# Mixed token pieces kept as 16-bit integers for the up stage, up-weight blocks one chunk later, second element's integers one chunk sooner

## The chip, the core and the metric

The kernel runs on one core of a Trainium2 chip. The time of a run is the device time of one execution in microseconds (us). The core has a matrix engine (TensorE, PE in the profile; its weight loads are shown as PEld), three elementwise engines (VectorE = DVE, ScalarE = ACT, GpSimd = POOL), and SyncE (SP), which in this kernel does hardly more than issue DMA transfers. The data sits in SBUF (128 partitions), matmul results in PSUM banks, everything large in DRAM (HBM).

## The reference, cut to what matters

Sixteen sequences ("elements") of 512 tokens, 512 features each. A cross attention comes first and its result is added to x; then a quantized feed-forward network follows, whose hidden size is 1536:

```
x = x + attention(layernorm(x), ctx)
h = act_qdq(layernorm(x))                      # 16-bit integers times one scale for the whole tensor
up   = act_qdq(h @ lpbq_dequant(w_up).T)       # weights: 4-bit integers, one scale per block of 32
gate = act_qdq(h @ lpbq_dequant(w_gate).T)
sig  = fixed_qdq_u16(sigmoid(gate))            # multiples of 1/65536
gate = act_qdq(gate * sig)
o    = act_qdq(gate * up)
x = x + o @ lpbq_dequant(w_down).T

act_qdq(x): scale = max(max|x| / 32767, 1e-12); round(x / scale), clipped to 16 bits, times scale
```

Each `act_qdq` needs the largest magnitude of its whole tensor before the first element can be rounded. This is why the network cannot be run in one pass: gate has to be finished over all elements before its integers exist, and so on.

## The kernel before, in words

There are five stages: attention (to 992 us), gate (to 1559), up (to 2120), a short turn in which the scales of o are found (to 2160), and down (to the end).

**Pieces.** The integers of the tokens have 16 bits, more than a matmul takes in one go at full speed. So `Tokens` cuts a tile of 128 features by 512 tokens (one of four, `d`, of an element) into three `Pieces`: `hi` (the integer rounded to a multiple of 256, `split_high`, L705), `lo` (the rest) and `mix` (`hi` minus a multiple of `lo`; both in `split_low`, L707 to L711). Weights are likewise kept as three pieces, made once and stored in DRAM. The product is made from three passes: the mixed pieces (`begin`, L769), then after one scaling of the sums in PSUM on ACT (`divide`, L775) the low and high pieces (`rest`, L725).

**Chunks and steps.** The gate and the up stage each have 96 chunks: sixteen elements by six chunks `f` of 256 hidden features. A chunk is 24 matmuls, 8 in `begin` and 16 in `rest`. One `step(i)` writes the order by hand for PE, DVE, ACT and POOL:

```python
nxt.begin()              # PE: 8 matmuls of chunk i+1
chunks[i - 1].out(...)   # ACT: copy sums to t, SyncE: store t
before()                 # ACT: gate integers (up stage)
nxt.divide()             # ACT
middle()
chunks[i].rest()         # PE: 16 matmuls of chunk i
after()
```

The sums have three PSUM buffers, the tile `t` three; two further PSUM banks ("tp") are for transposes. SyncE is not in the hand-written order: its order of issues is planned at compile time, from when the planner takes each DMA to be ready, and SyncE then issues in that order, one after the other, each when what it waits for has come.

**Gate stage** (the loop over `b` and `f` after `chunks[0].divide()`). The tokens of element b+1 are got ready while element b is multiplied: `load` brings the rows of x (one element earlier, at its f=2), `normalize` (POOL, at its f=4), then, in element b, `quantize` (L828 to L832: ACT makes the integers `xi`, one DMA transposes them into the integer tile `xq`, another, issued right behind, stores `xq` to DRAM as `xq_d` for the up stage; f=0, for element 1 f=2), the high splits on POOL (f=1, 2), the low splits with the mixes on DVE (f=2, 3, 4). There are two integer tiles `xq`, and two sets of four pieces. Elements 1 to 12 also prepare one block of up weights each (`up_weight`: load at f=0, quantize at f=1, transposes on PE at f=2 and the rest of the split at f=3), and elements 2, 5, 8 and 11 begin one block of down weights (`down_weight`, L844; load at their f=4, quantize at f=5, then three transposing steps in the next element at f=0 to 3). Within one `after`, the down block's step stands ahead of the up block's. Both take one of the two tp banks per step, and a bank is free again when the DVE step L169 of `rest()` of the same turn has read it; `rest()` of one down step is called at the next one.

In this text a gate element is counted from 0. An up block's own four steps start inside element b at the step with f=0; PE runs `after` of a step behind the 16 matmuls of that step, so the transposes of f=2 stand behind the rest of chunk 2 and ahead of the begin of chunk 4.

**Up stage** (the loop over `k`). The elements are taken in the order 15, 14, 0, 1, ... 13: the pieces of 15 and 14 are still in SBUF. For all others the integers come back from `xq_d` (L1041, at f=4 two elements ahead) and are split again during the element before: high on POOL ahead of the step, low and mix on DVE behind it, one `d` in each of f=0 to 3. That makes 56 low splits and 56 mixes. Alongside runs the gate work, per chunk: load gate sums `gt` (L975, seven buffers), integers and sigmoid on ACT (L953, L959), two DVE steps that make the rounded sigmoid and the product p (`times`, L963, L964), its store `p_d` (L982), the product with `t` on POOL (L987), two reductions on DVE (L991 and L792). So SyncE has three transfers of 512 KB in each chunk: `gt` in, `p_d` and `u_d` (the sums of the up product) out. At k=1 the scale of the gate is found, at k=3 (L1062) the scale of p, with a few small steps on ACT and DVE.

Of the kernel before, what the change touches and what calls it, by code (L numbers as in the profile page):

```python
# [9 lines left out]
F32 = mybir.dt.float32  # L10
F32R = mybir.dt.float32r
I32 = mybir.dt.int32
I16 = mybir.dt.int16
# [8 lines left out]
P = 128  # L22
# [31 lines left out]
def tile_xattn_ffn(  # L54
# [16 lines left out]
    nc = tc.nc  # L71
    B, S, D = x.shape
    SK = cx.shape[1]
    FF = w_gate.shape[0]
    ND = D // P
    NF = FF // P
    NQ = S // P
# [7 lines left out]
    dram = ctx.enter_context(tc.tile_pool(name="dram", bufs=1, space=DRAM))  # L85
# [8 lines left out]
    max_x = const.tile([P, B * NQ], F32, name="max_x")  # L94

    xq_d = [dram.tile([P, NQ, ND, P], I16, name=f"xq_{b}") for b in range(B)]

    wg_d, wu_d, wd_d = (dram.tile([P, NF, 3, D], F32, name=f"w{k}_d") for k in "gud")
    x1_d = [dram.tile([NQ, P, D], F32, name=f"x1_{b}") for b in range(B)]
# [22 lines left out]
    class WeightBlock:  # L122
# [13 lines left out]
        def quantize(self):  # L136
            pool, I, tag, nm = self.pool, self.I, self.tag, self.nm
            nb = I // WBLOCK
            wb = self.wt.rearrange("p (n k) -> p n k", k=WBLOCK)
            s = pool.tile([P, nb], F32, tag=f"s_{tag}", name=f"ws_{nm}", bufs=1)  # L140
            nc.vector.tensor_reduce(s, wb, AX.X, ALU.max, apply_absolute_value=True)
            nc.vector.tensor_scalar(s, s, 1.0 / 7.0, SCALE_MIN, ALU.mult, ALU.max)
            r = pool.tile([P, nb], F32, tag=f"r_{tag}", name=f"wr_{nm}", bufs=1)
            nc.vector.reciprocal(r, s)
            q = pool.tile([P, I], I16, tag=f"q_{tag}", name=f"wq_{nm}", bufs=1)
            qb = q.rearrange("p (n k) -> p n k", k=WBLOCK)
            nc.vector.tensor_tensor(
                qb, wb, r.unsqueeze(2).to_broadcast([P, nb, WBLOCK]), ALU.mult
            )
            nc.vector.tensor_scalar(q, q, 7.0, -8.0, ALU.min, ALU.max)  # L150
            nc.vector.tensor_tensor(
                wb, qb, s.unsqueeze(2).to_broadcast([P, nb, WBLOCK]), ALU.mult
            )
# [550 lines left out]

        engine.tensor_scalar(as_runs(p.hi, q), q, TO_256, TO_256, ALU.add, ALU.subtract)  # L705

    def split_low(p, q):  # L707
        nc.vector.tensor_tensor(  # L708
            as_runs(p.lo, q), q, as_runs(p.hi, q).bitcast(F32), ALU.subtract
        )  # L710
        nc.vector.scalar_tensor_tensor(  # L711
            out=p.mix, in0=p.lo.bitcast(F32), scalar=-SPLIT, in1=p.hi.bitcast(F32),
            op0=ALU.mult, op1=ALU.add,
        )

    def as_runs(t, q):
        return t if t.shape == q.shape else t.rearrange("p (q t) -> p q t", t=q.shape[-1])
# [21 lines left out]
    with ExitStack() as gu:  # L739
        ps_mm = gu.enter_context(tc.tile_pool(name="psf_mm", bufs=3, space=PSUM))  # L740
        xpool = gu.enter_context(tc.tile_pool(name="ff_x", bufs=1))
# [3 lines left out]
        class Tokens:  # L745


            def __init__(self, b, nm):
                self.b, self.nm, self.p = b, f"{nm}_{b}", []
                self.q = xpool.tile([P, NQ, ND, P], I16, tag="xq", name=f"xq_{self.nm}", bufs=2)  # L750

            def high(self, d, engine):
                self.p.append(Pieces(xpool, "x", [P, S], 8, f"{self.nm}_{d}"))
                split_high(self.p[d], self.q[:, :, d, :], engine)

            def low(self, d):
                split_low(self.p[d], self.q[:, :, d, :])

        class Chunk:
            def __init__(self, w, x, b, f):  # L760
# [35 lines left out]
        wp = wprep.__enter__()  # L796
# [9 lines left out]
        xs = {0: Tokens(0, "g")}  # L806
# [18 lines left out]
        def quantize(b):  # L825

            xi = wp.tile([P, NQ * D], I16, tag="xi", name=f"xi_{b}")
            nc.scalar.activation(  # L828
                xi, xs[b].x1.rearrange("p q d -> p (q d)"), AF.Copy, scale=r_x
            )  # L830
            nc.sync.dma_start_transpose(xs[b].q.rearrange("p q d t -> p (q d) t"), xi)
            nc.sync.dma_start(xq_d[b], xs[b].q)  # L832


        def up_weight(o):
# [24 lines left out]
        load(1)  # L860
        normalize(1)
        wg.load(range(4, NF))
        nc.sync.dma_start(xq_d[0], xs[0].q)
        nc.vector.tensor_scalar(s_xw, s_x, WHOLE, None, ALU.mult)

        order = [B - 1, B - 2, *range(B - 2)]
        chunks = [Chunk(wg, b, b, f) for b in range(B) for f in range(N2)]
        chunks += [Chunk(wu, b, b, f) for b in order for f in range(N2)]
        xu = {}
# [28 lines left out]
        for b in range(B):  # L898
            for f in range(N2):
                i = b * N2 + f  # L900

                def middle():
                    if f == (0 if b else 2) and b + 1 < B:
                        quantize(b + 1)

                def after():

                    if b == 0:
                        high = {3: ((0, nc.vector), (1, nc.gpsimd), (2, nc.gpsimd)), 4: ((3, nc.vector),)}
                        low = {3: (0,), 4: (1, 2, 3)}  # L910
                    else:
                        high = {k: ((2 * k - 2, nc.gpsimd), (2 * k - 1, nc.gpsimd)) for k in (1, 2)}
                        low = {2: (0, 1), 3: (2,), 4: (3,)}
                    if b + 1 < B:
                        for d, engine in high.get(f, ()):
                            xs[b + 1].high(d, engine)
                        for d in low.get(f, ()):
                            xs[b + 1].low(d)
                    if i > 0:
                        chunks[i - 1].largest(max_g, **size)  # L920
                        chunks[i - 1].largest(top_g)
                    if f == 2 and b + 2 < B:
                        load(b + 2)
                    if f == 4 and b + 2 < B:
                        normalize(b + 2)
                    if f == 0 and 1 <= b <= NF:
                        ups.extend(up_weight(b - 1))
                    if f == 4 and b % 3 == 2 and b < NF:
                        downs.extend(down_weight(b // 3))
                    for jobs in (downs, ups):  # L930
                        if jobs:
                            jobs.pop(0)()
                    if b == B - 1:
                        wu.load((0,) if f == 0 else (2 * f - 1, 2 * f))

                if b == B - 1 and f == 0:
                    wprep.__exit__(None, None, None)
                step(i, None, middle, after)


# [80 lines left out]
        for k in range(NCH):  # L1021
            i, n = NCH + k, k // N2
            f = k % N2

            def before():
                for j in sig[k]:
                    gates[j].sigmoid()

            def middle():
                for j in sig[k]:  # L1030
                    gates[j].sigmoid2()

            def after():
                if k == 0:
                    wu.load((NF - 1,))
                if splits:
                    xu[order[n + 1]].low(f)
                if n + 2 < B and f == ND:
                    b = order[n + 2]
                    xu[b] = Tokens(b, "u")  # L1040
                    nc.sync.dma_start(xu[b].q, xq_d[b])  # L1041
                if n == B - 1:
                    wd.load((0,) if f == 0 else range(max(1, 2 * f - 3), 2 * f - 1), (0,))

            splits = 1 <= n < B - 1 and f < ND
            if splits:
                xu[order[n + 1]].high(f, nc.gpsimd)
            for j in times[k]:
                gate_times(j)
            while multiplied:  # L1050
                gate_rows(multiplied.pop(0))
            step(i, before, middle, None)
            for j in times[k]:
                gate_product(j)
                multiplied.append(j)
            if k == 0:
                chunks[NCH - 1].largest(max_g, **size)
                chunks[NCH - 1].largest(top_g)
            else:
                chunks[i - 1].largest(max_u, **size)  # L1060
            if k == 1:
                m_g = over_all([max_g, top_g], "g")  # L1062
                s_g, r_g = scale_of(m_g[:, 0:1], s_xw, "g")
                nc.vector.tensor_tensor(r_g, r_g, s_xw, ALU.mult)
            if k == 3:


                nc.vector.tensor_copy(m_p, m_g[:, 1:2])
                top = Gate(m_p, 1, "top")
                top.sigmoid()  # L1070
                top.sigmoid2()
                top.times()
                scales_of_p()
                low = small.tile([P, 1], F32, name="low")
                nc.vector.tensor_scalar(low, m_p, P_LEAST * U16_ONE, None, ALU.is_lt)
                nc.gpsimd.iota(first_i, pattern=[[0, 1]], base=0, channel_multiplier=NF)
                nc.vector.tensor_copy(first_row, first_i)
            if k == 0:
                for j in range(3):
                    gate_load(j)  # L1080
            gate_load(k + 3)
            after()

        for j in times[NCH]:
# [45 lines left out]
    with ExitStack() as dn:  # L1130
# [38 lines left out]
        class Unit:  # L1169
# [10 lines left out]
            def fetch(self, g, more=""):  # L1180
                self.q[g] = factors(self.b, self.h, 4 * g, more)
# [139 lines left out]
        with tc.If(nc.values_load(again[0:1, 0:1], min_val=0, max_val=1)):  # L1321
            every = [(b, h, f) for b, h in units for f in range(0, NF, 4)]
            max_p = small.tile([P, len(every)], F32, name="max_p")
            for i, unit_f in enumerate(every):
                p, _ = factors(*unit_f)
# [77 lines left out]
```

## Time and profile before

The median of three runs is 2714.57 us (2711.21 to 2718.05). The profiled execution took 2716.41 us.

| profiled execution | us |
|---|---|
| its time | 2716.41 |
| span, first to last instruction | 2714.6 |
| attention, to 992.0 | 992.0 |
| gate, 992.0 to 1559.4 | 567.4 |
| up, 1559.4 to 2120.2 | 560.8 |
| turn, 2120.2 to 2160.0 | 39.8 |
| down, to the end | 554.6 |

| busy us in the stage | PE | DVE | ACT | POOL | share of the DMA engines |
|---|---|---|---|---|---|
| gate | 546.6 | 416.0 | 234.0 | 285.1 | 0.67 |
| up | 546.9 | 513.6 | 390.9 | 365.5 | 0.85 |
| down | 537.5 | 447.1 | 232.0 | 396.4 | 0.67 |

The first table is read from the begins of the stages in the timeline, the second from the view of windows, which gives the busy time of each engine in a stretch, the clock that was granted to TensorE in it, and what the DMA engines moved. The view of waits lists, for each engine and line, how long it stood idle and whose end released it; the lines of SyncE in it (SPq) are the waits of the queue of DMA issues. A line number is one of the kernel before.

### The profile page before, as it was taken

To read this page: it belongs to the slowest core of one execution; us is meant where nothing else is said; L and a number is where in the kernel's file an instruction comes from. 1 tells how busy PE (TensorE), PEld (TensorE's weight loads), DVE (VectorE), ACT (ScalarE), POOL (GpSimd) and SP (SyncE) were. 2 spreads that over 40 slices of the span, in tenths; PEclk is the share of its full clock that TensorE was granted. 3 is DMA by queue.
4 is the path that set the end of the run, shared out by engine and by line. 5 is a ranking of instruction groups with operands and counts; after the bars stand their busy time and mean duration, and the time that the engine had idled before them with its cause. 6 is when DMAs were issued, how large, how long until landed. Compare 5 with 4: busy or idle time off the path is not lost. (4 is left out here: it accounts for less than half of the span.)

```text
span 2714.6 us, 30451 instructions
## 1 busy us (share of the span) xinstructions
PE 2586.2 (95%) x10934; PEld 1692.6 (62%) x10934; DVE 2067.9 (76%) x2671; ACT 1092.3 (40%) x1182; POOL 1603.8 (59%) x1011
## 2 busy tenths in 40 slices
PE   8899999999999879999999999999999389999999
PEld 4334434333343347787787878777777278788787
DVE  4667766776777557887878579999998678888886
ACT  1221222222222214444444467766766444444443
POOL 4466665655665145556556147777665367777775
PEclk9999999999999989999999999999999799999999
DMA  4011121111111057666666688888888967777773
GB/s 158 15 62 47 66 89 47 47 54 47 47 68 38 16 202 215 213 194 218 213 198 194 221 296 291 277 276 290 283 279 270 362 236 252 249 255 250 250 248 140
DMA packets 264399, 486.85 MB, mean 179 GB/s; under 512 B 47024, under 2 KB 65584, under 8 KB 264240
## 3 DMA queue, kind: packets, MB, share of 16 engines
q1 hardware_dynamic: 264080, 484.31, 52.7%
q8 instruction: 87, 1.43, 0.2%
q14 instruction: 72, 0.59, 0.1%
q0 software_dynamic: 160, 0.52, 0.0%
HBM read 255.66 MB, written 221.25 MB: 176 GB/s over the span
## 5 line engine op out<-in xcount | busy, mean ns | idle before, releaser
L705 POOL TENSOR_SCALAR oh_d<-oq_d 128x512 fp32r<-128x512 int16 x190 | 398.5, 2119 | 156.1 <-DVE oq_d L1193 155.8
L987 POOL TENSOR_TENSOR po<-gt,t_wu 128x1024 f32<-128x1024 f32 x96 | 231.5, 2411 | 242.6 <-DVE gt L964 127.4
L384 ACT COPY ao<-pv 128x512 f32<-128x512 f32 x64 | 37.5, 586 | 505.3 <-PE pv L375 505.3
L308 PE MATMUL qp<-xnT,wq_sb 128*128 128x512 f32 x512 | 236.4, 604 | 0.0
L404 PE MATMUL op<-wo_sb,ao 128*128 128x512 f32 x512 | 232.1, 601 | 0.0
L792 DVE TENSOR_REDUCE max_g<-t_wg 128x1 f32<-128x1024 f32 x96 | 116.8, 1216 | 135.3 <-ACT t_wg L787 135.3
L705 POOL TENSOR_SCALAR xh_g<-xq_g 128x512 fp32r<-128x512 int16 x60 | 121.6, 2046 | 164.4 <-DMA xq_g<-xi 158.5
L769 PE MATMUL mm_wg<-xm_g,wg 128*128 128x512 f32 x768 | 203.8, 408 | 9.3 <-DMA wg<-wg_d 4.6
L1210 PE MATMUL dn_d<-wd,om_d 128*128 128x512 f32 x768 | 194.6, 402 | 18.2 <-DMA wd<-wd_d 6.4
L725 PE MATMUL mm_wg<-xl_g,wg 128*128 128x512 f32 x768 | 208.0, 393 | 0.0
L725 PE MATMUL mm_wg<-xh_g,wg 128*128 128x512 f32 x768 | 205.7, 390 | 0.0
L220 POOL TENSOR_TENSOR rt_q<-rt_q,sin_q 128x512 f32<-128x512 f32 x64 | 81.4, 1272 | 202.5 <-DVE rt_q L217 202.5
L1193 DVE SCALAR_TENSOR_TENSOR oq_d<-pq_d,r_o,uq_d 128x1024 int16<-128x1024 int16 x96 | 128.0, 1333 | 82.0 <-ACT uq_d L1146 82.0
L725 PE MATMUL mm_wu<-xl_u,wu 128*128 128x512 f32 x672 | 185.8, 398 | 2.2 <-ACT mm_wu L775 2.2
L1210 PE MATMUL dn_d<-wd,ol_d 128*128 128x512 f32 x768 | 184.6, 389 | 0.4 <-ACT dn_d L1222 0.4
L1210 PE MATMUL dn_d<-wd,oh_d 128*128 128x512 f32 x768 | 184.5, 389 | 0.0
L1210 PEld LDWEIGHTS dn_d<-wd,om_d 128*128 128x128 f32 x768 | 144.2, 192 | 63.4 <-DVE om_d L711 20.3
L769 PE MATMUL mm_wu<-xm_u,wu 128*128 128x512 f32 x672 | 173.1, 399 | 11.0 <-ACT t_wu L787 6.8
L335 DVE TRANSPOSE_TENSOR_REDUCE mt<-st 128x32 f32<-128x1024 f32 x128 | 151.7, 1224 | 39.1 <-PE st L329 38.9
L725 PE MATMUL mm_wu<-xh_u,wu 128*128 128x512 f32 x672 | 180.1, 390 | 0.0
L308 PEld LDWEIGHTS qp<-xnT,wq_sb 128*128 128x128 f32 x512 | 92.1, 189 | 137.8 <-issue 111.2
L769 PEld LDWEIGHTS mm_wg<-xm_g,wg 128*128 128x128 f32 x768 | 148.4, 196 | 42.9 <-DVE xm_g L711 8.1
(248 smaller groups left out, 5586.1 us busy)
## 6 DMA issues: line engine op xcount, KB each, us to landing
g_d<-t_wg SPq DMA_DIRECT2D x96, 512.0 KB, 3.4
gt<-g_d SPq DMA_DIRECT2D x96, 512.0 KB, 4.5
u_d<-t_wu SPq DMA_DIRECT2D x96, 512.0 KB, 5.8
p_d<-gt SPq DMA_DIRECT2D x96, 512.0 KB, 5.1
p<-p_d SPq DMA_DIRECT2D x96, 512.0 KB, 4.9
u<-u_d SPq DMA_DIRECT2D x96, 512.0 KB, 5.9
xt<-in_x_dram SPq DMA_DIRECT2D x16, 1024.0 KB, 5.3
x<-xt SPq DMA_DIRECT2D x16, 1024.0 KB, 4.3
```

Source lines behind the costliest of these rows:

```text
L220: nc.gpsimd.tensor_tensor(v(t), v(t), sin, ALU.mult)
L308: nc.tensor.matmul(ps, lhsT=wq_sb[:, d, ts(g, P)], rhs=self.xnT[:, d, :], start=(d == 0), stop=(d == ND - 1),)
L335: nc.vector.tensor_reduce(self.mt[:, 2 * i : 2 * i + 2, :NB], self.st[i].rearrange("p h (c j) -> p h c j", j=DK), AX.X, ALU.max, apply_tra ...
L384: nc.scalar.copy(self.ao[:, g, :], pv)
L404: nc.tensor.matmul(ps, lhsT=self.ao[:, g, ts(q, P)], rhs=wo_sb[:, g, :], start=(g == 0), stop=(g == NG - 1),)
L705: engine.tensor_scalar(as_runs(p.hi, q), q, TO_256, TO_256, ALU.add, ALU.subtract)
L725: nc.tensor.matmul(ps[:, j, :], lhsT=lhs(j, i)[k], rhs=rhs(j, i)[k], start=(k == 0 and i == 0), stop=(k != 1 and i == n - 1), skip_group_c ...
L769: nc.tensor.matmul(self.ps[:, j, :], lhsT=lhs(j, d), rhs=self.x.p[d].mix, start=(d == 0), stop=(d == ND - 1), skip_group_check=True,)
L792: nc.vector.tensor_reduce(maxes[:, i : i + 1], self.t, AX.XYZ, ALU.max, **how)
L987: nc.gpsimd.tensor_tensor(flat(g.po), flat(g.tile), flat(c.t), ALU.mult)
L1193: nc.vector.scalar_tensor_tensor(out=oq.rearrange("p f t -> p (f t)"), in0=pq, scalar=r_o, in1=uq, op0=ALU.mult, op1=ALU.mult,)
L1210: nc.tensor.matmul(self.ps[j], lhsT=self.p[f // 2].all()[k][:, f % 2, ts(j, P)], rhs=wd.made[f][k], start=(k == 0 and f == 0), stop=(k != ...
```

## The change

The change has these parts:

- `split_low` gets a flag, and its second instruction becomes `split_mix`. In the up stage the mixes are not computed by DVE any more. In the gate stage `short_mixes` (ACT, f=2 and 3 of each element but the last two) writes the mixed pieces divided by 256 as 16-bit integers into a tile `xn`, which is stored to DRAM (`xn_d`, 512 KB per element). In the up stage `fetch` loads `xn` behind `xq`, and `mix` (ACT, in the middle of the steps f=0 to 3) multiplies it by 256 back into the mixed piece. `xn` has one buffer in each stage.
- The integer tile `xq` has one buffer instead of two.
- The store of `xq` is a method `keep`, called in `after` at f=1 (for element 1 at f=2) instead of right behind the transposing DMA, and not for elements 14 and 15.
- Element 1 is quantized at f=1 of element 0 instead of f=2, and two of its low splits instead of one are made at f=3.
- The up-weight block starts at f=1 instead of f=0, so each of its four steps stands one chunk later.
- The scale of p is found at k=2 instead of k=3.

```diff
-    def split_low(p, q):
+    def split_low(p, q, mix=True):
         nc.vector.tensor_tensor(
             as_runs(p.lo, q), q, as_runs(p.hi, q).bitcast(F32), ALU.subtract
         )
+        if mix:
+            split_mix(p)
+
+    def split_mix(p):
         nc.vector.scalar_tensor_tensor(
             out=p.mix, in0=p.lo.bitcast(F32), scalar=-SPLIT, in1=p.hi.bitcast(F32),
...
-                self.q = xpool.tile([P, NQ, ND, P], I16, tag="xq", name=f"xq_{self.nm}", bufs=2)
+                self.q = xpool.tile([P, NQ, ND, P], I16, tag="xq", name=f"xq_{self.nm}", bufs=1)
...
-            def low(self, d):
-                split_low(self.p[d], self.q[:, :, d, :])
+            def low(self, d, mix=True):
+                split_low(self.p[d], self.q[:, :, d, :], mix)
+            def keep(self):
+                nc.sync.dma_start(xq_d[self.b], self.q)
+            def short_mixes(self, pool, ds):
+                if ds[0] == 0:
+                    self.n = pool.tile([P, ND, S], I16, tag="xn", name=f"xn_{self.nm}", bufs=1)
+                for d in ds:
+                    nc.scalar.mul(self.n[:, d, :], self.p[d].mix.bitcast(F32), 1.0 / 256.0)
+                if ds[-1] == ND - 1:
+                    nc.sync.dma_start(xn_d[self.b], self.n)
+            def fetch(self):
+                nc.sync.dma_start(self.q, xq_d[self.b])
+                self.n = xpool.tile([P, ND, S], I16, tag="xn", name=f"xn_{self.nm}", bufs=1)
+                nc.sync.dma_start(self.n, xn_d[self.b])
+            def mix(self, d):
+                nc.scalar.mul(self.p[d].mix, self.n[:, d, :], 256.0)
...
             nc.sync.dma_start_transpose(xs[b].q.rearrange("p q d t -> p (q d) t"), xi)
-            nc.sync.dma_start(xq_d[b], xs[b].q)
...
-        nc.sync.dma_start(xq_d[0], xs[0].q)
+        xs[0].keep()
...
                 def middle():
-                    if f == (0 if b else 2) and b + 1 < B:
+                    if f == (0 if b else 1) and b + 1 < B:
                         quantize(b + 1)
+                    if f in (2, 3) and b < B - 2:
+                        xs[b].short_mixes(wp, ((0, 1), (2, 3))[f - 2])
...
-                        low = {3: (0,), 4: (1, 2, 3)}
+                        low = {3: (0, 1), 4: (2, 3)}
...
+                    if f == (1 if b else 2) and b + 1 < B - 2:
+                        xs[b + 1].keep()
...
-                    if f == 0 and 1 <= b <= NF:
+                    if f == 1 and 1 <= b <= NF:
                         ups.extend(up_weight(b - 1))
...
             def middle():
                 for j in sig[k]:
                     gates[j].sigmoid2()
+                if splits:
+                    xu[order[n + 1]].mix(f)
...
                 if splits:
-                    xu[order[n + 1]].low(f)
+                    xu[order[n + 1]].low(f, False)
...
-                    nc.sync.dma_start(xu[b].q, xq_d[b])
+                    xu[b].fetch()
...
-            if k == 3:
+            if k == 2:
                 nc.vector.tensor_copy(m_p, m_g[:, 1:2])
                 top = Gate(m_p, 1, "top")
```

More of the change, by code (lines that the diff above doesn't have):

```diff
@@ L96, in tile_xattn_ffn @@
     xq_d = [dram.tile([P, NQ, ND, P], I16, name=f"xq_{b}") for b in range(B)]
+    xn_d = [dram.tile([P, ND, S], I16, name=f"xn_{b}") for b in range(B)]
     wg_d, wu_d, wd_d = (dram.tile([P, NF, 3, D], F32, name=f"w{k}_d") for k in "gud")
```

## The prediction

> **What bounds the kernel now.** I read the page's slices first, of forty 68 us each:
>
> ```profile
> PE   8899999999999879999999999999999389999999
> ...
> DVE  4667766776777557887878579999998678888886
> ...
> DMA  4011121111111057666666688888888967777773
> ```
>
> Gate is slices 15 to 23 (992 to 1559 us), up 24 to 31 (to 2120), down the last nine. In both of the first two PE counts as 90% busy; DVE is at 70% in the gate stage and over 90% in the first half of up, where DMA is above 80%. A busy PE may be a slow one, so I took the begins of the chunks from the timeline. An unhindered chunk (24 matmuls) lasts 5.44 us, an element of six 32.6, and a gate element that also turns one up block 33.1. Up needs 561 us where 96 chunks of 5.44 are 522. The waits of PE, then of SyncE from 1710 to 2100 us (time, times, longest):
>
> ```profile
> PE tp_wu L159 <- issue: 16.1, 4, 4.3
> ...
> PE mm_wu L769 <- ACT t_wu L787: 6.8, 10, 1.3
> ...
> PE mm_wg L769 <- DVE xm_g L711: 4.4, 4, 2.0
> ```
> ```profile
> SPq L975 <- DMA p_d<-gt: 241.3, 65, 5.9
> ```
>
> **Gate.** The wait of 16.1 falls in elements 3, 6, 9 and 12, which turn a down block as well. The timeline of element 3, then two windows (busy of PE, PEld, DVE, ACT, POOL, granted clock, DMA share, GB/s):
>
> ```profile
> 1121.95 0.60 PE L159 MATMUL tp_wd<-ident,wt_wd 128*128 128x128 f32 x4
> ...
> 1125.20 0.69 DVE L169 TENSOR_TENSOR wt_wd<-tp_wd,wt_wd 128x512 f32<-128x512 f32 x1
> ...
> 1125.99 1.09 PE L159 MATMUL tp_wu<-ident,wt_wu 128*128 128x128 f32 x4 [3.44 <-issue]
> ...
> 1126.73 3.76 PE L769 MATMUL mm_wg<-xm_g,wg 128*128 128x512 f32 x8
> ```
> ```profile
> 1126.60:1134.60 8.00, 8.00 (x28) 6.43 (x27) 7.57 (x9) 3.03 (x4) 4.06 (x3) 0.69 0.66 217
> 1140.00:1173.00 33.00, 33.00 (x149) 27.35 (x148) 24.02 (x28) 14.51 (x14) 16.02 (x9) 1.00 0.63 200
> ```
>
> The reader is to see that PE turns a down part at 1121.95, then stands 3.44 us before the up block's turn (both at f=2), whose PSUM bank DVE frees only at 1125.89 (L169: 1125.20 and 0.69), behind the low splits. After it the granted clock is 0.69 and the next chunk takes 7.8 us. The four elements last 40.8, 40.6, 41.8 and 40.3, 163.5 together.
>
> **Up.** SyncE issues the stores and loads of a chunk in one fixed turn:
>
> ```profile
> 1745.70 0.57 SPq L975 DMA_DIRECT2D gt<-g_d  x1
> 1746.36 0.56 SPq L982 DMA_DIRECT2D p_d<-gt  x1
> 1747.02 0.57 SPq L788 DMA_DIRECT2D u_d<-t_wu  x1
> 1751.63 0.57 SPq L975 DMA_DIRECT2D gt<-g_d  x1
> ```
> ```profile
> 1700.00:1800.00 100.00, 98.79 (x428) 79.31 (x427) 98.94 (x97) 71.82 (x71) 73.58 (x31) 1.00 0.82 275
> 2000.00:2100.00 100.00, 96.66 (x407) 73.87 (x405) 86.84 (x86) 68.68 (x68) 60.58 (x26) 1.00 0.81 271
> ```
>
> The gt load waits until the p store issued one turn earlier has landed, since there are seven gt buffers. A turn is (2095.1-1710.5)/65 = 5.92 us, 0.48 over PE's 5.44, 31 us over the 65. DVE made that p some ten us before its store was issued (multiplied at 1865.7, issued 1876.6). And DVE's share falls from 98.94 to 86.84 of 100 while the turn stays as it is: the loop of issues sets the pace, not DVE.
>
> **The change, part by part.** The profiled execution took 2716.4 (span 2714.6), 1.8 above the median 2714.6; the sum starts from 2716.4.
>
> *Up block one chunk later.* Each block moves whole: one load of 256 KB, six DVE instructions of quantizing (3.1 us), four transposes, and after them two on DVE (0.68, 0.69), one on ACT (0.63), one on POOL (1.7) and three stores. At f=2 PE then turns only a down part; the block's turn comes at f=3, where the down block only ends its split, and its bank was freed a chunk before. An element of this kind should take 33.1 plus three down turns of .36 to .5, 34.3: 163.5-4*34.3 = 26 us saved. Bounds: 0 (another wait takes its place) and 26; the 16.1 alone if the slow clock stays. I take 26, since the 33.1 us of a neighbour with a clock of 1.00 is the nearest row. POOL's last step of the block (1.7) now stands behind its normalize (8.3); POOL is busy 16 of 33, so nothing, and 1.7 a block if that cover were gone. SyncE issues the load and the stores 5.4 us later, in a stage where nothing of the chain waits for them.
>
> *Stored integers in the gate stage.* 56 ACT copies f32 to 16-bit: not in the trace; the f32 copies of this size are 0.63, a 16-bit one 0.70, so 39 us in 14 elements on an engine 14.5 of 33 busy, between the division and the next copy of t: nothing; 0.7 each on PE at worst. The 14 stores of 512 KB meet a DMA share of 0.63: nothing. The xq stores move on SyncE from behind the transposing DMA to f=1 or 2, and two fall away: nothing. From element 2 on the single buffer asks that the transposing DMA (f=0) follow the last low split of the element before (f=4, one chunk earlier) and its xq store (f=1): both are done, so nothing.
>
> *Element 1 sooner.* begin(1) is 6.0 us late now, for DVE's mixes. Its ACT quantize at 1013.6 could start at 1009. But with one integer buffer the transposing DMA needs the xq store of element 0 landed (1018.66, behind 24 weight loads), 4 to 5 us later than the ACT step allows: gain eaten. Bounds -6 and +3; I take 0, as the last mix comes out at 1032.3 against 1032.6.
>
> *DVE relief in up.* 56 mixes of 0.90 leave DVE (50.3 us) and 56 go to ACT, of 0.65 each, between the two rows above (4.31 busy per 5.44 chunk, so 4.96 where it falls: hidden, but with 0.5 to spare). The loop of issues is untouched by it: 0. Bounds: 0 and -31 (the whole excess). One chunk of 9.67 in the first split element waits 2.6 for a DVE mix; its 4.2 go, and come back as waiting in the loop.
>
> *Loads of the integers.* Turns with an xq load last 6.00 and the next 6.19, others 5.84: 0.16+0.35 = 0.5 us a load. 14 more of the same 512 KB: +7. Bounds 0.1 and 2.0 each (two turns reached 7.87), +1 to +26. More traffic needs 1.748 MB in 5.44 us, 321 GB/s in such a chunk, under the 362 that slice 34 shows. *One xq buffer:* the fetch waits for the last low split, which the second buffer spares it now. The earliest fetch still lands in time (issued 1730.1, landed 1737.0, POOL's split at 1739.8). Later ones slip: issued at 1872.2 or after, landing 6.4 later, where POOL starts at 1874.2. Taken so for each element, eight loads land 0.4 to 4.6 us after POOL's present start, 26.5 together. p's ten us and 4 to 6 us of lead of gt hide that; without cover, see below. Bunching after it +2.
>
> *Top gate at k=2*: two ACT steps (0.28, 0.29), a table load of 1.28 and small DVE steps stand one chunk sooner, where SyncE's loop has not begun to wait; -2 (0 to -5.4, a chunk).
>
> By the Trainium skill, "DMA: Bandwidth & Descriptors", "Anatomy of one DMA — SWDGE (gpsimd) path", a transfer costs about 2.0 us plus bytes over 436 GB/s; an estimate from it gives 1.2 us of moving for each integer load and +17 instead of +7, though the path named there is not the one used here, and the turns above show 0.5.
>
> Sum: 2716.4-26+0+0+7+2-2 = 2697.4, less the 1.8 to the median: **2696**. Its own range goes two thirds of the way to the bounds of the loads (+1, +26) and of element 1 (-6, +3): 2688 to 2711.
>
> **The rivals.**
>
> *Up is relieved as well.* DVE at 98.9 of 100 in the first half speaks for it; or, with DVE lighter, the planned order puts p's store ahead of the gt load, and the loop loses its waits of up to 5.9. Against: p is ready ten us early, and DVE's share falls with no gain in pace. All 31 gone gives 2716.4-26-31-1.8 = 2658, half of it 2673; about 2666. The Trainium skill, "Perfetto Trace Analysis", "Identifying the Most-Contended Engine", says to optimise the engine of highest occupancy: that is DVE in this stage, and by it this case, 2658, would be the likeliest. The trace does not agree: DVE's share falls by 12 of 100 while the turn stays at 5.92.
>
> *Slower: one buffer of integers.* The late loads pass through POOL and DVE to PE: +26.5, and xn, queued 1.4 us behind xq, holds up the ACT mixes eight times, +11.5; with the 7 of the loads 2716.4-26+26.5+11.5+7-1.8 = 2734 (2722 to 2734). It decides from 2.6 us per element. For it: POOL has 73.6 of 100 busy, ACT 71.8. Against: the leads above.
>
> *New waits in the gate.* The block's quantize ends about 26.0 us into an element, PE wants the turn at 27.1: 1.1 us of room. If DVE's order uses it up, half of the 26 is lost: 2709.
>
> *The early element delays instead*, with its store queued behind the weight loads: +3 at most, inside the first range.
>
> **How the numbers follow.** Forecast .55, up relieved .22, new waits .12, slower .11. 0.3% is 8.1 us (2706.4 and 2722.7), about what a measurement here can tell from no change. Faster holds nearly all of the first two and a little of the third, .78; same .11; slower .11. For the range I leave out about one in ten on each side: up to the start of the slow case, 2722, and down to the middle of the relieved one, 2662.
>
> **What would show it.** Right: no wait of tp_wu in the gate elements 3, 6, 9, 12 and 34 to 35 us for each; begin(1) late as before; SyncE's gt loads still waiting for p's stores, at a turn of 5.9 to 6.0; DVE in up down to 80 of 100. Wrong: a turn near 5.5 (relief), or waits of POOL's high splits or of ACT's mixes for the integers, passed on to PE (slower), or a wait of PE for the block's quantized weights.

## The result and the profile after

The changed kernel takes 2694.59 us (median of four runs, 2691.84 to 2695.72) against 2714.38 for the kernel before; the ratio is 0.9925 with a 95% interval of 0.9908 to 0.9942. The prediction of 2696 lies 1.4 us from it. The gain, however, is in another stage than the one predicted. By the begins of the chunks in the two traces:

| us, profiled executions | before | after |
|---|---|---|
| to the first begin of the gate stage | 992.1 | 993.4 |
| gate stage, to the first begin of the up stage | 567.2 | 568.6 |
| up stage, to the begin of its last chunk | 550.0 | 526.3 |
| from there to the end | 605.3 | 604.0 |
| span | 2714.6 | 2692.3 |

The gate stage, for which 26 us had been promised, is 1.4 us longer. The up stage, for which +7 had been written, is 23.7 us shorter.

**Gate after.** The waits of PE in the changed kernel (engine, tile and line, releaser: us in all, times, longest):

```profile
PE tp_wu L160 <- DVE wt_wu L152: 11.2, 3, 5.1
...
PE tp_wd L160 <- DVE wt_wd L152: 7.1, 4, 2.4
```

The old wait of 16.1 for a PSUM bank is gone, as predicted, and 18.3 us of other waits have come: PE now waits for the quantized weights themselves. The three waits for the up block are in elements 4, 7 and 10, those behind an element with a down block; the four for the down block in elements 3, 6, 9 and 12. Element 3 went from 40.8 to 38.7 us, but element 4 from 33.1 to 37.3, and so on: 6 went from 40.6 to 36.3, 7 from 33.1 to 40.3. The timeline of element 4 shows the order on DVE that does it (start, duration, engine, line, operation; idle time before it and its releaser):

```profile
1157.59 7.62 POOL L706 TENSOR_SCALAR xh_g<-xq_g 128x512 fp32r<-128x512 int16 x4 [9.66 <-PE mm_wg L795]
...
1159.55 1.09 DVE L709 TENSOR_TENSOR xl_g<-xq_g,xh_g 128x512 fp32r<-128x512 int16 x1 [5.83 <-POOL xh_g L706]
...
1165.44 0.68 DVE L142 TENSOR_REDUCE ws_wu<-wt_wu 128x16 f32<-128x512 f32 x1
...
1168.21 0.69 DVE L152 TENSOR_TENSOR wt_wu<-wq_wu,ws_wu 128x512 f32<-128x512 int16 x1
...
1168.96 0.66 PE L160 MATMUL tp_wu<-ident,wt_wu 128*128 128x128 f32 x4 [2.39 <-DVE wt_wu L152]
```

DVE stood idle for 5.83 us ahead of the first low split (L709), which waits for POOL's high split (L706), which started when the transposing DMA landed at 1157.43. The quantizing (L142 to L152) is written behind the two low splits of f=2 and could not start in that gap, though its weights had landed at 1153.69. One chunk earlier, at f=1, there is no low split ahead of it.

The transposing DMA was itself late, and again through the moved block. POOL makes the last piece of the up block of element 3 (L172) behind its normalize (L846); SyncE has the store of that piece ahead of the transposing DMA in its order, and waits 5.6 us for it:

```profile
1138.39 8.27 POOL L846 TENSOR_SCALAR x1t<-x1t,ln_mv,ln_rstd 128x512 f32<-128x512 f32 x4
1146.62 1.30 POOL L172 TENSOR_TENSOR wa_wu<-wt_wu,wt_wu 128x512 f32<-128x512 f32 x1
```
```profile
1147.95 0.32 SPq L861 DMA_DIRECT2D wu_d<-wa_wu  x1
...
1151.85 3.91 SPq L857 DMA_TRANSPOSE xq_g<-xi  x1
```

So the transposing DMA is issued 12.6, 15.5 and 14.2 us into the elements 4, 7 and 10. In 5, 8 and 11 it is issued 10.45 us into the element, the quantizing ends 26.2 us into it, and PE does not wait.

The down block's wait comes from DVE's order as well: its quantizing ends 12.5 to 13.4 us into the element instead of 10.2 to 10.6. The up block's last two steps (0.68 and 0.69) now stand ahead of it, and so does what the later quantizing (3.3) put off; the experiments below tell which of the two it is. After the waits of 2.4 us and more PE's granted clock is low again, as it was before: 0.76 in the 7.2 us from 1169.3. After the three waits of 1.5 to 1.6 us, those for the down block in elements 6, 9 and 12, it stays at 1.00.

**Up after.** Two windows (us, then busy time and count of PE, PEld, DVE, ACT, POOL, then granted clock, DMA share, GB/s), and SyncE's longest wait from 1710 to 2080 us:

```profile
1700.00:1800.00 100.00, 100.00 (x443) 82.81 (x442) 96.80 (x88) 81.14 (x87) 72.97 (x32) 1.00 0.90 311
...
2000.00:2080.00 80.00, 78.72 (x342) 63.17 (x341) 74.97 (x66) 60.47 (x64) 51.53 (x22) 1.00 0.89 306
```
```profile
SPq L1004 <- DMA p_d<-gt: 199.3, 59, 5.8
```

The elements of the up stage are counted on from the gate's sixteen, 16 to 31. Numbers 17 to 25 now last 32.64 us each, the unhindered time; from 26 on they last 33.3 to 34.5. In the kernel before they lasted 33 to 37 from number 20 on. SyncE still waits in most chunks for a p store to land. But its order is not the same around the loads of an element's integers:

```profile
1754.14 0.57 SPq L1004 DMA_DIRECT2D gt<-g_d  x1
1754.80 0.56 SPq L1011 DMA_DIRECT2D p_d<-gt  x1
1755.46 0.57 SPq L814 DMA_DIRECT2D u_d<-t_wu  x1
1756.08 1.28 SPq L778 DMA_DIRECT2D xq_u<-xq  x1
1757.45 1.24 SPq L780 DMA_DIRECT2D xn_u<-xn  x1
1758.78 0.58 SPq L1011 DMA_DIRECT2D p_d<-gt  x1
1759.41 0.67 SPq L814 DMA_DIRECT2D u_d<-t_wu  x1
1760.48 0.57 SPq L1004 DMA_DIRECT2D gt<-g_d  x1
1761.14 0.75 SPq L1011 DMA_DIRECT2D p_d<-gt  x1
```

Behind the two loads a p store (1758.78) stands ahead of the next gt load (1760.48), where the kernel before always had gt first. For two turns of each element the gt load then needs a p store behind which one more has been issued. Of the 66 gt loads from 1710 to 2080 us, 21 are of this kind; 7 of them do not wait for a p store, and the mean wait of all 21 is 1.5 us. The other 45 all wait, 3.7 us on the mean. Counted over the whole order, the p stores issued trail the gt loads by six from the 24th gt load on in the kernel before; with seven buffers this means each load waits for the store just issued. In the changed kernel they trail by five in at least two of six turns, up to the last loads of integers.

### The profile page after: what moved, and what is told of

It reads as the page before. It is cut to its first block, busy times and chain, and to the rows that moved or that the text cites. A ratio compares the mean times of both kernels' runs of the same rounds, so it can differ in the third digit from the quotient of the medians.

```text
span 2692.3 us, 30619 instructions
## 1 busy us (share of the span) xinstructions
PE 2570.3 (95%) x10934; PEld 1695.1 (63%) x10934; DVE 2052.8 (76%) x2615; ACT 1146.8 (43%) x1294; POOL 1580.3 (59%) x1011
## 5 line engine op out<-in xcount | busy, mean ns | idle before, releaser
L706 POOL TENSOR_SCALAR oh_d<-oq_d 128x512 fp32r<-128x512 int16 x190 | 398.5, 2120 | 154.9 <-DVE oq_d L1224 154.7
L706 POOL TENSOR_SCALAR xh_g<-xq_g 128x512 fp32r<-128x512 int16 x60 | 116.6, 1966 | 171.0 <-DMA xq_g<-xi 155.5
L1241 PE MATMUL dn_d<-wd,om_d 128*128 128x512 f32 x768 | 195.5, 405 | 17.6 <-DMA wd<-wd_d 6.4
L405 PEld LDWEIGHTS op<-wo_sb,ao 128*128 128x128 f32 x512 | 93.8, 191 | 123.6 <-issue 112.2
```

The lines of the kernel that those rows point to most:

```text
L405: nc.tensor.matmul(ps, lhsT=self.ao[:, g, ts(q, P)], rhs=wo_sb[:, g, :], start=(g == 0), stop=(g == NG - 1),)
L1241: nc.tensor.matmul(self.ps[j], lhsT=self.p[f // 2].all()[k][:, f % 2, ts(j, P)], rhs=wd.made[f][k], start=(k == 0 and f == 0), stop=(k != ...
```

## The experiments: the gate stage

In the table and below, "gate" and "up" are the stages as bounded above, from the profiled execution of each kernel; the ratio is to the kernel before, measured on the same chip in the same series.

| kernel | median us | ratio, 95% interval | gate | up |
|---|---|---|---|---|
| before | 2714.4 | | 567.2 | 550.0 |
| changed | 2694.6 | 0.9925 [0.9908, 0.9942] | 568.6 | 526.3 |
| before, blocks one chunk later | 2715.5 | 1.0000 [0.9990, 1.0009] | 566.5 | 547.4 |
| changed, blocks at the old place | 2691.6 | 0.9917 [0.9900, 0.9933] | 567.5 | 526.2 |
| changed, only the turn later | 2669.7 | 0.9829 [0.9809, 0.9849] | 542.7 | 525.8 |
| before, only the turn later | 2689.8 | 0.9905 [0.9890, 0.9920] | 542.4 | 549.3 |
| before, program's DMA order | 2716.9 | 1.0012 [1.0002, 1.0021] | 567.6 | 551.4 |
| changed, mixes on DVE again | 2696.7 | 0.9934 [0.9917, 0.9950] | 569.7 | 532.4 |
| changed, without the loads of mixes | 2716.9 | 1.0005 [0.9995, 1.0016] | 567.4 | 545.5 |
| changed, without stored mixes | 2720.5 | 1.0016 [1.0005, 1.0028] | 567.3 | 547.4 |
| changed, program's DMA order | 2684.3 | 0.9887 [0.9871, 0.9904] | 569.0 | 518.1 |
| changed, element 0 stored first | 2694.9 | 0.9925 [0.9910, 0.9940] | 569.5 | 526.7 |
| changed, three edits | 2655.9 | 0.9777 [0.9764, 0.9790] | 542.7 | 518.1 |

The two stage columns come from one execution of each kernel. The three kernels whose up stage is that of the kernel before show 547.4 to 550.0 there, the four whose up stage is that of the changed kernel 525.8 to 526.7, so a difference of less than 3 us between stages tells nothing.

**Before, with the blocks one chunk later and nothing else.**

```diff
-                    if f == 0 and 1 <= b <= NF:
+                    if f == 1 and 1 <= b <= NF:
                         ups.extend(up_weight(b - 1))
```

> The kernel before with one edit: up-weight blocks start one chunk later. Theory A (formed from the profile of the changed kernel): moving the block trades the wait for the PSUM bank for waits on DVE's quantizing, in the elements with a down block and in the ones behind them; the gate stage stays at 567 us, within 6 of it, and the time at 2714, within 6. Theory B (the prediction's): the move alone saves 26 us of the gate stage (541), and something else in the change took it away; time 2688.

Measured: gate 566.5, ratio 1.0000. PE's waits of this kernel are those of the changed one:

```profile
PE tp_wu L159 <- DVE wt_wu L151: 10.5, 3, 4.9
...
PE tp_wd L159 <- DVE wt_wd L151: 7.1, 4, 2.2
```

So the move alone makes the new waits, and is worth nothing. No other part of the change took the 26 us away.

**Changed, with the blocks back.** The same edit undone.

> The changed kernel with the up-weight blocks back at their old chunk. Theory A: the old waits of 16 us in elements 3, 6, 9, 12 return and the new ones of 18 go; gate stage 568, within 6; time 2694, within 6. Theory B: the gate stage gets 26 us longer (594), time 2720.

Measured: gate 567.5, time 2691.6, and the old wait:

```profile
PE tp_wu L160 <- issue: 16.0, 4, 4.2
```

Both ends agree: the place of the block as a whole does not matter, since a late bank is exchanged for a late quantizing.

**Only the turn later.** A block is loaded and quantized at the old place, f=0 and f=1, then does nothing for a chunk, and is turned at f=3 and ended at f=4 as in the change:

```diff
-                    if f == 1 and 1 <= b <= NF:
+                    if f == 0 and 1 <= b <= NF:
...
-                w.load, w.quantize, lambda: rest.append(w.turn(0)), lambda: rest.pop()()
+                w.load, w.quantize, lambda: None, lambda: rest.append(w.turn(0)), lambda: rest.pop()()
```

> The changed kernel with an up-weight block loaded at f=0 and quantized at f=1, as before, and turned at f=3 and ended at f=4, as in the change. Theory A (old place: waits for the bank; new place: waits for the quantizing, which stands behind the low splits): neither wait is left except that for the down block's quantizing (7); gate stage 545 to 553, time 2671 to 2679. If the waits only move again: gate stage 560 or more.

Measured: gate 542.7, 25.9 us less than the changed kernel, and no wait for tp_wu or tp_wd among PE's. Elements 3, 6, 9 and 12 last 34.5 to 34.6 us, 4, 7 and 10 last 33.1. The waits for the down block, which I had thought would stay, went too: with the up block's quantizing back at f=1 the down block's ends 10.19 us into the element again, although the up block's last two steps are still at f=4. So it was the place of the quantizing that put DVE back, in both kinds of element. The transposing DMA of elements 4, 7 and 10 is as late as in the changed kernel (13.4, 15.1 and 13.3 us into the element), which costs PE nothing now that the quantizing stands ahead of the low splits. The same idle step in the kernel before (without the first edit, as its blocks start at f=0 anyway):

> The kernel before with the blocks quantized at f=1 as before, but turned at f=3. If the prediction's 26 us for the bank's wait were right and only the quantizing's place spoiled them: gate stage from 567 to 541 to 543, time 2688 to 2692. If another part of the change is needed for it: gate stage 555 or more.

Measured: gate 542.4, 24.8 less, time 2689.8. The 26 us were there to be had, by a version of the move that keeps the quantizing where DVE has room.

## The experiments: the up stage

**Before, with the up stage's DMAs in the order of the program.** SyncE is added to the engines in hand-written order from the start of the up stage on; p's store, u's store and the gt load of a step then follow the code, and the p stores trail the gt loads by four.

```diff
         ap = gu.enter_context(tc.tile_pool(name="ff_act", bufs=2))
+        gu.enter_context(tc.manual_schedule(
+            engines={ENG.PE, ENG.DVE, ENG.Activation, ENG.Pool, ENG.SP}))
```

> The kernel before with SyncE's issues of the up stage in the order of the program (each gt load then has two turns for the p store it waits for, where the planned order left it one). Theory C (the prediction's: the order of issues paced the up stage, DVE did not): up stage, first begin to the begin of its last chunk, from 550 to about 525 us, time about 2690. Theory D (DVE paced it: 34.5 us of work for an element of 32.6): up stage 540 to 550, time 2705 to 2714.

Measured: up 551.4, no gain. The prediction's theory falls in this form: the wait for p's landing is gone, and PE is not faster. The windows and the waits of this kernel, of PE and then of SyncE (1710 to 2100 us):

```profile
1800.00:1900.00 100.00, 95.60 (x412) 78.00 (x411) 98.79 (x92) 69.74 (x70) 69.52 (x29) 0.98 0.83 289
1900.00:2000.00 100.00, 96.15 (x422) 78.56 (x421) 97.72 (x91) 70.10 (x69) 67.61 (x29) 1.00 0.83 289
```
```profile
PE mm_wu L769 <- DVE xm_u L711: 19.9, 14, 2.6
```
```profile
SPq L983 <- DVE gt L965: 220.1, 68, 6.9
```

DVE is busy for 98 of 100 us all through the stage (in the kernel before it fell to 86.8 in the last third), PE waits once in each of the 14 elements that are split for a mix, 19.9 us in all, and SyncE waits for DVE. With the first bound removed, DVE was the next one, and it holds the stage at the same length to 1.4 us. It is PE's waits that show this; a share of 98 alone would not, as the last run of this section shows.

**Changed, with the mixes on DVE again.** DVE writes each mix once more over what ACT has written. ACT's work and the loads stay. The order of issues is planned anew with the edit, and it is a better one: ahead of 34 of the 66 gt loads from 1710 to 2080 us the p stores trail by five or four, where the changed kernel has 21 of 66.

```diff
-                    xu[order[n + 1]].low(f, False)
+                    xu[order[n + 1]].low(f)
```

> The changed kernel with the 56 mixes of the up stage made by DVE once more, over what ACT has written, so DVE's load is back while ACT's mixes and the extra loads stay. Theory D: up stage from 526 back to 548 or more, time 2716 or more. Theory C: up stage 526 to 532, time 2695 to 2700.

Measured: up 532.4, between the two expectations. Elements last 33.5 us, evenly to the end. The lines of the window, of PE's waits and of SyncE's (1710 to 2080 us) say which bound it is:

```profile
1900.00:2000.00 100.00, 98.17 (x430) 80.31 (x430) 98.02 (x96) 78.55 (x84) 73.37 (x31) 1.00 0.90 318
```
```profile
PE mm_wu L795 <- DVE xm_u L716: 9.9, 14, 1.9
```
```profile
SPq L1004 <- DMA p_d<-gt: 106.8, 33, 5.0
```

DVE, with PE waiting for its mixes; SyncE's wait for p's landing is half of what it was, and none of the 34 loads waits for it. So DVE with the mixes needs 33.5 us for an element, 0.9 more than PE. Most of the 24 us stays without the relief. The 6 us to the changed kernel (532.4 against 526.3) are not the price of the mixes alone, since the order differs too.

**Changed, with the loads of the mixes left out but the first.** ACT does the same work on the tile of the first element; SyncE's planned order is then that of the kernel before, with p trailing gt by six in every turn from the 18th gt load on.

```diff
             def fetch(self):
                 nc.sync.dma_start(self.q, xq_d[self.b])
-                self.n = xpool.tile([P, ND, S], I16, tag="xn", name=f"xn_{self.nm}", bufs=1)
-                nc.sync.dma_start(self.n, xn_d[self.b])
+                if not kept:
+                    kept.append(xpool.tile([P, ND, S], I16, tag="xn", name=f"xn_{self.nm}", bufs=1))
+                    nc.sync.dma_start(kept[0], xn_d[self.b])
+                self.n = kept[0]
```

> The changed kernel with the loads of the stored mixes left out except the first (ACT multiplies the first element's mixes each time, so the up sums of later elements are wrong): DVE is relieved as in the change, but SyncE's planned order has each gt load right behind the wait for the p store just issued, as the kernel before, where the changed kernel has an element's worth of two turns with one p store more in hand. Theory E (the order with that one store more in hand is what gave most of the gain): up stage from 526 to 540 to 548 us, time 2708 or more, in spite of 7 MB less to move. Theory F (DVE's relief gave it): up stage 522 to 527, time 2690 to 2695.

Measured: up 545.5, time 2716.9. Fewer bytes, a relieved DVE, and nearly all of the gain is gone. Elements last 32.6 us up to element 21 and 33.5 to 36.5 after it, once the lead of the stage's start is used up. SyncE's wait (1710 to 2080 us), and a window, in which DVE has room again:

```profile
SPq L1008 <- DMA p_d<-gt: 231.7, 63, 5.5
```
```profile
1900.00:2000.00 100.00, 98.10 (x408) 73.89 (x407) 89.70 (x79) 73.91 (x80) 66.36 (x30) 1.00 0.85 282
```

So the gain needs the planned order that came with the 14 loads. Relief of DVE alone is worth 4.5 us at most (550.0 to 545.5, of which 4.2 are in element 18, and the times show no gain: ratio 1.0005). Loads and a better order with DVE's mixes are worth 17.6 (550.0 to 532.4), relief and the changed kernel's order together 23.7. The changed kernel's own order with DVE's mixes was not run, so the exact shares stay open.

**Changed, without stored mixes.** No stores, loads or ACT work for them; DVE makes the mixes, with the one buffer of integers and all the moved steps.

```diff
-                    xu[order[n + 1]].low(f, False)
+                    xu[order[n + 1]].low(f)
...
-                if splits:
-                    xu[order[n + 1]].mix(f)
```

> The changed kernel without stored mixes at all (no ACT work for them, no stores, no loads; DVE makes the mixes as before), but with one buffer of integers, the later blocks and the other moved steps. Both E and F: up stage 546 to 552, as before, and time 2712 to 2718. Theory G (the rival of the prediction, one buffer of integers is late for POOL): up stage 560 or more, time 2726 or more.

Measured: up 547.4, gate 567.3; the ratio of 1.0016 [1.0005, 1.0028] is 4 us above the kernel before, within the 0.3% that I took as telling nothing. One buffer of integers costs nothing that the stage shows, so the slower rival's mechanism is not there; and the steps that were moved besides the mixes give nothing.

**Changed, with the program's DMA order.** The edit shown above, on the changed kernel.

> The changed kernel with SyncE's issues of the up stage in the order of the program, where each gt load has two turns for its p store. E: the elements of more than 33 us at the end of the stage go; up stage 523 to 526, time 2688 to 2694. If it is above 530, the order of the program has a fault of its own (in the kernel before DVE's low splits took 1.44 us with it against 1.02).

Measured: up 518.1, of which 95 chunks of 5.44 are 516.8. Time 2684.3. From element 17 on every element lasts 32.64:

```profile
1900.00:2000.00 100.00, 100.00 (x443) 82.84 (x442) 99.33 (x87) 81.85 (x88) 73.91 (x32) 1.00 0.93 328
```

With both bounds gone, each of which gave next to nothing in this place (551.4 with the order alone, 545.5 with the relief alone), PE does not wait at all, while the window moves 328 GB/s with extra loads in it. DVE is busy for 99 of 100 us here, and SyncE's longest wait is for DVE (197.9 us from 1710 to 2080), as in the kernel before with this order: neither shows by itself that DVE holds the pace.

## The experiments: element 1, and the sum

**Changed, element 0's integers stored ahead of the gate weights.**

```diff
+        xs[0].keep()
         load(1)
         normalize(1)
         wg.load(range(4, NF))
-        xs[0].keep()
```

> The changed kernel with element 0's integers stored ahead of the loads of gate weights. The prediction's reading of element 1 (the transposing DMA waits for that store, which stands behind the weights): the transposing DMA is issued 4 to 6 us sooner, element 0 and 1 together last 69 to 70 us instead of 74.0, time 2690, within 3. If the DVE work or the input of element 1 is late anyway: 73 to 74 us, time 2694.

Measured: elements 0 and 1 together 73.5 us against 74.0, time 2694.9: the gain did not come. The transposing DMA was issued 6.3 us sooner (1013.94 against 1020.24), 4.9 us counted from the begin of the stage, as expected. But it took 7.84 us instead of 4.45, beside the loads of the gate weights that it used to follow, and landed at 1021.78 against 1024.69. That run's gate stage had begun 1.4 us sooner, so 1.5 remain, and the last mix came 1.2 sooner. What would bring element 1 in time is open; no further order was tried.

**Three edits together**: only the turn later, the program's DMA order, and element 0 stored first.

> The changed kernel with three edits together: blocks quantized at f=1 and turned at f=3, the up stage's DMAs issued in the order of the program, and element 0's integers stored ahead of the loads of the gate weights (so that the transposing DMA of element 1 does not wait for them). Gate stage 543 less 4 to 5 in element 0 and 1: 538; up stage 518; time 2657, within 6. If the two bounds of the up stage and the blocks' waits were not independent, 2665 or more.

Measured: 2655.9 us, ratio 0.9777 [0.9764, 0.9790] to the kernel before; gate 542.7, up 518.1. The two gains add: 568.6-542.7 = 25.9 and 526.3-518.1 = 8.2 make 34.1, and the median is 38.7 under the changed kernel's. The profiled executions lie 41.6 apart: the gate stage began 2.2 us sooner in this one, and what lies behind the begin of the last up chunk was 5.3 us shorter (598.7 against 604.0), for which I have no cause. The 4 to 5 us of the third edit did not come, as above. This version is faster than both kernels.

## Why the prediction was right, and where it was not

The time was right to 1.4 us, and the two largest terms of its sum were both wrong, by 27 and 31 us in opposite directions. That they cancel is luck: the mechanism forecast for the gate stage did not give its gain, and the one held to be unlikely for the up stage did. Point by point:

- *Up block one chunk later, -26.* Wrong: measured +1.4 for the stage, and 1.0000 for this part alone. The step that failed is "At f=2 PE then turns only a down part; the block's turn comes at f=3": it followed the bank and treated the rest of the block as free of cost. The rival "New waits in the gate" had half of the mechanism, with half the loss and a chance of .12, and the wait for the quantized weights was among the signs of being wrong. Its 1.1 us between quantizing and turn did hold in elements 5, 8 and 11. They did not in 4, 7 and 10, by two terms that the prediction put at nothing: POOL's last step "now stands behind its normalize", and SyncE's issues come later "in a stage where nothing of the chain waits for them". The transposing DMA of the next element stood behind that store on SyncE, and the quantizing stood behind the low splits that wait for that DMA; PE waited 11.2 us. No run moved that store alone; with the quantizing back in its place the late DMA costs nothing. The other half I had not seen at all: the quantizing at f=2 puts DVE back ahead of the down block's quantizing, and PE waited 7.1 us there. The size of 26 itself was right, as the kernels with only the turn moved show (24.8 and 25.9; 34.5 to 34.6 us for an element forecast at 34.3).
- *Stored integers in the gate stage, 0.* Right: the stage is 568.6 with them and 567.3 without.
- *Element 1, 0.* Right: 74.0 us for elements 0 and 1, before and after, with the transposing DMA behind the store of element 0 as said. The reason was half of it, as the run above shows.
- *DVE relief in up, 0.* Nearly right by itself, 4.5 us at most in the run that kept the old order, but the sentence under it failed: "The loop of issues is untouched by it: 0". The loop is planned anew for each kernel, and the 14 loads shifted it so that it waited less. The rival "Up is relieved as well" names this ("the planned order puts p's store ahead of the gt load") with the wrong cause: it is not the lighter DVE that turns the order, since the kernel with DVE's mixes back has such turns too, more of them even, and the one without the loads has none. DVE's share, forecast at 80 of 100, is 94 to 97: the stage goes faster, and the mean low split is longer (1.31 us against 1.01, see the end).
- *"The loop of issues sets the pace, not DVE."* Half right. The falling share of DVE did show a second bound, but not that DVE was free: with the loop's wait removed, PE waited for DVE's mixes and the stage stayed at 551. DVE with the mixes takes 33.5 us for an element of 32.6, or 35.0 where a low split meets POOL's product (below); the loop took 35.3 in elements 22 to 30. The rule of the Trainium skill that the prediction set against this ("Perfetto Trace Analysis", "Identifying the Most-Contended Engine": optimise the engine of highest occupancy first) would have given the up stage's relief to DVE, and by itself that was worth 4.5 us of 32 at most; the trace agrees with it only once the order of the issues is mended as well.
- *Loads of the integers, +7, and bunching +2.* Wrong sign in the planned order, and no cost in the program's: 518.1 us with all of them. The 0.5 us per load was read from turns that were all waiting for a p store. The estimate of +17, from the Trainium skill's "DMA: Bandwidth & Descriptors", fell further still.
- *One buffer of integers.* Right: 0.
- *Top gate at k=2, -2.* Not seen: the first element of the stage lasts 34.0 in both.

## What to carry to other kernels

A step that makes PE wait for one of its inputs has others: before it is moved, look up what stands ahead of each of its parts on their own engines at the new place, and move only the part that was late. Where two bounds lie within a few per cent of each other, as DVE (33.5 to 35.0 us) and the queue of DMA issues (35.3) here, removing either shows next to nothing and says nothing against it; remove both in one run before either is given up. Take the bound from what PE waits for, not from a share of busy time: DVE stood at 98 where it held PE and at 99 where it did not. Where the order of a DMA queue is planned by a program, an edit anywhere can turn it, so compare that order first, by how many stores stand between a load and the one that it needs.

## What the runs showed of the hardware

DVE's low split (two inputs) waits for the end of POOL's product of two tiles (L987 in the kernel before) if it begins inside it. In the up stage of the changed kernel with the program's order (VectorE's and POOL's timelines):

```profile
1867.21 2.53 DVE L709 TENSOR_TENSOR xl_u<-xq_u,xh_u 128x512 fp32r<-128x512 int16 x1
...
1874.25 1.01 DVE L709 TENSOR_TENSOR xl_u<-xq_u,xh_u 128x512 fp32r<-128x512 int16 x1
```
```profile
1866.79 2.40 POOL L1017 TENSOR_TENSOR po<-gt,t_wu 128x1024 f32<-128x1024 f32 x1
...
1872.32 2.40 POOL L1017 TENSOR_TENSOR po<-gt,t_wu 128x1024 f32<-128x1024 f32 x1 [0.79 <-DVE gt L994]
```

The first low split began 0.42 us into a product, the second 1.93 us into the next one, and both ended 0.55 us behind the end of their product (1869.19 and 1874.72). So did all 56 low splits of this stage, within 0.01, and 54 of the 56 in the kernel before; the other two there met no product and took 0.68 and 0.82 us. In the kernel before none began early in a product and the mean was 1.01 us. In the program's order 13 of the 56 did, on both kernels, and took 2.5 to 2.9; the mean on the kernel before is then 1.38. That is 1.5 us of DVE in each element, as much as the kernel before with the program's order took more for an element (35.0 us) than the one with DVE's mixes back (33.5, with a mean of 1.02). The Trainium skill, "SBUF — State Buffer", "SBUF: two separate sides", says that VectorE and GpSimd share a pair of ports under an exclusive lock, which a VectorE operation with two SBUF inputs needs against a GpSimd operation that reads SBUF, and that the one that starts first keeps it for its whole instruction while the other is blocked; these lines agree with it.

A stop of PE of 2.4 us is enough for a slow chunk behind it: 7.5 us instead of 5.44 (and .5 for the turn) at a granted clock of 0.78 in element 3 of the changed kernel, 7.2 at 0.76 in element 4. The stops of 1.54 to 1.59 us in elements 6, 9 and 12 were followed by a clock of 1.00 and cost little more than themselves (36.3 us for the element against 34.5 to 34.6 without the stop); what happens between 1.6 and 2.4 these stops do not show. In all, 18.3 us of waits went with 25.9 of gate stage, so the view of waits alone shows too little.
